# A sum of squares on VectorE: one reduction over nine places in place of two additions in PSUM

## The chip, the cores and the metric

The kernel runs on one core of a Trainium2 chip. The metric is the device time of one execution in microseconds; it is compared by the median of several runs.

## The reference

One layer of a graph network: 12500 nodes with 96 features, 412500 directed edges sorted by their target, four attributes an edge. `_mlp` is a linear layer, ReLU, and a normalization over all rows, whose mean and variance are those of the whole column.

```python
def _mlp(h, W, b, gamma, beta):
    h = jax.nn.relu(h @ W + b)
    mu = jnp.mean(h, axis=0)
    var = jnp.mean(jnp.square(h - mu), axis=0)
    return gamma * (h - mu) * jax.lax.rsqrt(var + EPS) + beta

node_feat = _mlp(x, W_node, b_node, g_node, beta_node)
edge_feat = _mlp(edge_attr, W_edge, b_edge, g_edge, beta_edge)
row, col = edge_index[0], edge_index[1]
message = jnp.concatenate([x[row], x[col], edge_feat], axis=1)
message = _mlp(message, W_msg, b_msg, g_msg, beta_msg)
agg = jax.ops.segment_sum(message, col, num_segments=node_feat.shape[0])
return agg + node_feat          # then x = layernorm(x + this)
```

For the variance of the messages the kernel needs the sum of the squares of all 412500 messages, for each of the 96 features. That sum is what the change touches.

## The kernel before

Edges are handled in groups of 512 (4 tiles of 128 edges, `GT` = 4), and groups in blocks of four (`BG`). Before the main loop, tables are made (`x` times the source and target parts of `W_msg`, as `p_tab` and `q_tab`), the node part is computed and the edge attributes' statistics are taken. The main loop (in `fast`) takes one group at each step `k`; two steps make a pair. All engines' orders in it are written out by hand (`manual_schedule`), so each engine's queue is the order of the code.

A step, by engine:

- GpSimd (POOL) gathers the rows of `p_tab` for a later group, three or four indirect DMAs of 128 rows (`gather`, L226). It reuses the buffer of a pair of groups, and so waits for the pair's second message.
- TensorE (PE) makes the linear part of group `k + 2` into one of three PSUM banks (`linear`, L602, L606), and sums the messages of group `k - 2` by target (`sums`, L666). `edges` (L588) prepares the edge attributes of the next block.
- VectorE (DVE) adds the gathered rows to the linear part and applies the ReLU (`message`, L615, L618, L621). The result `h` lies in SBUF.
- In odd steps ScalarE (ACT) squares the two groups' messages into `sq`, 768 elements a partition (`squared`, L634); `sq` has two buffers, taken in turn. In the same step VectorE adds the squares of the pair *before* (`waiting`) to a running sum of 384 elements a partition in the PSUM bank `mixed` (`moments`, L640), one addition for each of the pair's groups.
- For some groups one of the four tiles is not gathered by GpSimd. Its columns are copied, each by an instruction of its own with an address from a register, out of `x`, which lies in SBUF (`copy_columns`, L745 on VectorE, L747 on ScalarE), into `xc`, and TensorE multiplies them. The addresses are brought into registers by `load_numbers` (L733), one TENSOR_LOAD for up to 20. A pair has three such lots on each of the two engines. VectorE's third lot is loaded between the two additions and copied behind them.
- For some others a tile's rows come by single DMAs from SyncE (SP) (`rows_of`, L433); SyncE also loads the edge attributes and the windows of `q_tab`.

VectorE's queue in an odd step is thus: message, load and copy of the second lot, first addition, load of the third lot, second addition, copy of the third lot. `places_of` (L628) then builds a comparison once a block from `rel` and `nodes_of`, which lies in the same PSUM bank as the running sum, and `add` (L685, L686) takes a finished block's sums over.

The instruction's names: `h` are messages, `z` the linear part, `pa` the sums by target, `pr` and `left` the edge part.

Once, after the loop's last pair, the running sum is reduced over its four tiles to `squares`, 96 elements a partition (L644), and `collect` (L651 to L656) adds what is left on GpSimd, halving the number of places by additions until one is left. A product with ones sums `squares` over the partitions (L839).

Of the kernel before, what the change touches and what calls it, by code (L numbers as in the profile page):

```python
# [12 lines left out]
F32 = mybir.dt.float32  # L13
# [101 lines left out]
def gnn(ctx, tc, t):  # L115
# [147 lines left out]
            for i in range(2):  # L263
                next(store)

    zero = const.tile([64, C], F32, name="zero")
    nc.vector.memset(zero, 0.0)
    nc.sync.dma_start(vec, t["vecs"])
    nc.sync.dma_start(w_node, t["L0_gnn_W_node"])
    nc.sync.dma_start(b_msg, t["L0_gnn_b_msg"])  # L270
# [187 lines left out]
    def fast(ring):  # L458
# [6 lines left out]
                return gather(g, pair[0][:, g % 2, :, :], int(g in by_row or g in by_column))  # L465

        with tc.manual_schedule(engines={ET.SP, ET.Pool}):
            nc.sync.dma_start(q_tab[:WM, :], zero[:WM])
            for r in range(WM + NN, WT, 64):
                n = min(64, WT - r)  # L470
                nc.sync.dma_start(q_tab[r:r + n, :], zero[:n])
            for i in range(2):
                next(store)
            places()
            for i in range(3):
                next(store)
# [12 lines left out]
            for _ in extra:  # L489
                pass  # L490
            got = {g: ahead_of(g) for g in range(SPILL, SPILL + RING)}
        with tc.tile_pool(name="fix", bufs=1) as fix, tc.tile_pool(name="msg", bufs=2) as work, \
                tc.tile_pool(name="msg_ps", bufs=2, space=PSUM) as ps:
            squares = fix.tile([P, C], F32, name="squares")
            mixed = ps.tile([P, GE], F32, name="mixed", bufs=1)
            wide_sq = mixed[:, :GT * C].rearrange("p (t c) -> p t c", c=C)
            nc.vector.memset(wide_sq, 0.0)
            nodes_of = mixed[:, GT * C:GT * C + BG * WN].rearrange("p (k w) -> p k w", w=WN)
            nc.vector.tensor_copy(nodes_of, iota)
            by_place = [ps.tile([P, GE], F32, name=f"pa{i}", bufs=1) for i in range(2)]  # L500
            total = fix.tile([C + 1, 1], F32, name="total")
# [65 lines left out]
            def convert(s):  # L567

                b = order[s]
                px = ps.tile([P, 2, GE], F32, name="pr", bufs=1)  # L570
                for i in range(BG):
                    for k in range(GT):
                        nc.tensor.transpose(px[:C, 0, k * P:(k + 1) * P], got[b * BG + i][:, k, :], ident)
                    xt = work.tile([P, 2, GT, C], F32, name="sq")[:C].rearrange("p g t c -> p (g t c)")[:, :GE]
                    nc.scalar.activation(xt, px[:C, 0, :], AF.Copy)
                    for k in range(GT):
                        nc.tensor.matmul(px[:, 1, k * C:(k + 1) * C], xt[:, k * P:(k + 1) * P], w_msg[:, 0, :],
                                         start=True, stop=True)
                    nc.vector.tensor_copy(got[b * BG + i], px[:, 1, :GT * C].rearrange("p (k c) -> p k c", c=C))
# [50 lines left out]
                    nodes_of[:, :m].unsqueeze(2).to_broadcast([P, m, GT, WN]), op=OP.is_equal)  # L630

            def squared(k, m=2, n=GT):
                sq = work.tile([P, 2, GT, C], F32, name="sq")
                nc.scalar.activation(sq[:, :m, :n, :], hb[k // 2 % HP][:, k % 2:k % 2 + m, :n, :C], AF.Square)  # L634
                return sq

            def moments(sq, at_last, between):

                for i in range(2):
                    nc.vector.tensor_tensor(wide_sq, wide_sq, sq[:, i, :, :], op=OP.add)  # L640
                    if i == 0:
                        between()
                if at_last:
                    nc.vector.tensor_reduce(squares, wide_sq.rearrange("p t c -> p c t"), axis=AX.X, op=OP.add)  # L644

            def collect(x, n, r=P):

                plus = nc.gpsimd.tensor_add
                whole = n if r == P else n - 1
                if r < P:  # L650
                    plus(squares[:r], x[:r, whole * C:n * C], squares[:r])  # L651
                while whole > 1:
                    half = whole // 2
                    plus(x[:, :half * C], x[:, :half * C], x[:, (whole - half) * C:whole * C])
                    whole -= half
                plus(squares, x[:, :C], squares)  # L656
# [69 lines left out]
            def load_numbers(k, part, engine):  # L726

                g, lo, hi = share(engine, k // 2 * XS + part)
                if g is not None:
                    assert engine not in held and hi - lo <= LOADED  # L730
                    if g not in apart:
                        apart[g] = work.tile([C, P], F32, name="xc", bufs=4)
                    _, held[engine] = nc.values_load_multi_w_load_instructions(  # L733
                        numbers[g][:, lo:hi], engines=[engine], min_val=FIRST, max_val=FIRST + 4 * (N - 1),
                        skip_runtime_bounds_check_because="they are nodes' numbers times four bytes, and FIRST")
# [16 lines left out]
            with tc.manual_schedule(engines={ET.SP, ET.Pool, ET.PE, ET.DVE, ET.Activation}):  # L752
# [13 lines left out]
                for k in range(last):  # L766
                    s, g = steps[k]
                    if g % BG == 0:
                        if s + 2 < len(order):
                            load(s + 2)  # L770
                            fetch(s + 2)
                    if k % 2 == 0 and k and pieces:
                        piece(pieces.pop(0))
                    apart_numbers(k)
                    if k % 2 == 0:
                        load_numbers(k, 0, ET.DVE)
                    message(k)
                    load_numbers(k, 1, ET.DVE) if k % 2 else copy_columns(k, 0, ET.DVE)
                    j = k - LATER - BG - 1
                    if k % 2:  # L780
                        load_numbers(k, 1, ET.Activation)
                        copy_columns(k, 1, ET.Activation)
                        now = squared(k - 1)
                        load_numbers(k, 2, ET.Activation)
                        copy_columns(k, 1, ET.DVE)
                        if waiting:
                            moments(waiting, k == last - 1, lambda: load_numbers(k, 2, ET.DVE))
                        waiting = now
                        copy_columns(k, 2, ET.DVE)
                        copy_columns(k, 2, ET.Activation)  # L790
                    if g % BG == 3 and s + 1 < len(order):
                        places_of(s + 1)
                    if j >= 0 and j % BG == 0:
                        add(j // BG, place(j // BG))
                    if k >= LATER:
                        sums(k - LATER)
                    if g % BG != 3 and s + 1 < len(order):
                        if g % 2:
                            edges(s + 1, 1)
                        else:  # L800
                            prepare(s + 1, g % BG // 2)
                    if g % BG == 3:
                        if s + 1 < len(order) and order[s + 1] < RAW:
                            convert(s + 1)
                        if s + 2 < len(order):
                            edges(s + 2, 0)
                    if k + ZB - 1 < n:
                        linear(k + ZB - 1)
                    if k % 2 == 0:
                        load_numbers(k, 0, ET.Activation)  # L810
                        copy_columns(k, 0, ET.Activation)
                    if g >= SPILL:
                        got[ahead] = ahead_of(ahead)
                        ahead += 1
                    apart_rows(k)
                    if k >= (max(column_start) + XN) // XS * 2 + 3 and loads:
                        y0s.append(residual(loads.pop(0)))
# [1 line left out]

                s, g = len(order) - 1, steps[last][1]  # L820
                m, r = NT - (g + 1) * GT, E - (NT - 1) * P
                collect(waiting.rearrange("p g t c -> p (g t c)"), 2 * GT)
                message(last)
                sq = [squared(last, 1, GT)]
                sums(last - 2)
# [1 line left out]
                unread(BUSY - 1)  # L827
                message(n - 1)
                sq.append(squared(n - 1, 1, m))
                collect(sq[0][:, 0, :, :].rearrange("p t c -> p (t c)"), GT)  # L830
                sums(last)
                at_end = place(s - 1), place(s)
                unread(1)
                collect(sq[1][:, 0, :, :].rearrange("p t c -> p (t c)"), m, r)
                add(s - 1, at_end[0])
                sums(n - 1)
                unread(1)
# [242 lines left out]
```

## Time and profile before

| | |
|---|---|
| median of 3 runs | 5507.97 us (5506.36 to 5508.45) |
| the profiled execution | 5517.2 us, its span 5515.5 us |
| mean granted TensorE clock | 0.624 |
| VectorE: busy, instructions | 3251.4 us (59%), 23435 |
| ScalarE: busy, instructions | 2835.6 us (51%), 16834 |
| L640, the additions | 802, 562 ns each |
| L745, VectorE's copies of columns | 20088, 185 ns each, from 1183 to 5363 us |

The profiled execution's time is its span and what lies around it. The page lists busy time, groups of instructions by line, and idle time with what ended it ("releaser"); "issue" is idle time in which an engine waited for nothing that the profile shows. "x20" counts instructions in a row.

### The profile page before, as it was taken

What the parts mean: (1) busy time and instruction counts of PE and PEld (TensorE: products, weight loads), DVE (VectorE), ACT (ScalarE), POOL (GpSimd) and SP (SyncE); (2) the same over time, 40 slices, a digit from 0 to 9 for tenths busy, and PEclk for the clock granted to TensorE, in tenths of its full rate; (3) what the DMA queues carried; (4) which work ended last, traced back from release to release, by engine and by line L of the source; (5) the groups of instructions that cost most, each with busy time, mean ns of one, the idle gap of its engine ahead of it and who ended that gap; (6) DMA issues with size and microseconds to landing.
All of it is one profiled execution on the core that took longest, in us unless ns stands there. A gap on an engine that the chain in (4) does not pass through costs nothing. (4 is left out here: it accounts for less than half of the span.)

```text
span 5515.5 us, 97011 instructions
## 1 busy us (share of the span) xinstructions
PE 3422.6 (62%) x17139; PEld 2745.4 (50%) x17139; DVE 3251.4 (59%) x23435; ACT 2835.6 (51%) x16834; POOL 2773.3 (50%) x2930
## 2 busy tenths in 40 slices
PE   3356674666666665666666666666666666666677
PEld 2133332455555555555555555555555555555556
DVE  1436666135556666666666666666666666666664
ACT  0225553135555565565555555555555655565552
POOL 5644445544445545545545545454555554545454
PEclk6555555565666666666666666666666666666657
DMA  6333332211111111111111111111111111111112
GB/s 165 117 89 70 67 75 64 60 51 29 35 33 40 39 37 42 39 38 39 37 40 32 39 39 40 39 38 39 40 40 40 39 39 38 33 39 39 38 49 83
DMA packets 201728, 274.41 MB, mean 50 GB/s; under 512 B 128941, under 2 KB 132166, under 8 KB 200218
## 3 DMA queue, kind: packets, MB, share of 16 engines
q0 software_dynamic: 92832, 142.78, 10.8%
q1 hardware_dynamic: 95304, 120.39, 7.9%
q10 hardware_dynamic: 12960, 4.93, 0.4%
q14 instruction: 494, 4.05, 0.2%
q8 instruction: 138, 2.26, 0.2%
HBM read 221.63 MB, written 46.23 MB: 49 GB/s over the span
## 5 line engine op out<-in xcount | busy, mean ns | idle before, releaser
L226 POOL DMA_INDIRECT pg<-p_tab,src x2837 | 2690.7, 948 | 2634.1 <-DVE h L621 1230.7
L747 ACT ACTIVATE xc<-big 96x4 uint8 x15624 | 1802.8, 192 | 1357.1 <-issue 1337.3
L745 DVE COPY xc<-big 96x4 uint8 x20088 | 1767.7, 185 | 1076.1 <-issue 1047.4
L602 PE MATMUL z<-rhs,left 128*128 128x96 f32 x6446 | 1449.4, 397 | 1392.9 <-remote 1015.3
L602 PEld LDWEIGHTS z<-rhs,left 128*128 128x128 f32 x6446 | 1318.1, 302 | 1784.5 <-remote 1227.1
L666 PE MATMUL pa<-at,h 128*97 128x80 f32 x6446 | 1005.0, 321 | 42.2 <-issue 42.1
L666 PEld LDWEIGHTS pa<-at,h 128*97 128x97 f32 x6446 | 959.5, 242 | 45.8 <-issue 45.7
L615 DVE CUSTOM_DVE_ANT_0 h<-z,pg 128x384 f32<-128x384 f32 (+1 forms) x690 | 348.2, 505 | 340.0 <-remote 130.1
L588 PE MATMUL pr<-ea,we 7*127 7x512 f32 x1380 | 458.5, 744 | 114.7 <-DMA ea<-rel_d 42.5
L596 ACT ACTIVATE left<-pr 127x1024 f32<-127x1024 f32 x403 | 404.4, 1003 | 236.2 <-remote 130.4
L634 ACT ACTIVATE sq<-h 128x768 f32<-128x768 f32 x404 | 339.7, 841 | 360.7 <-DVE h L621 182.4
L385 PE MATMUL pr<-ea,wide 10*128 10x512 f32 x1212 | 393.3, 1072 | 181.2 <-ACT r L389 80.3
L389 ACT ACTIVATE r<-pr 128x1024 f32<-128x1024 f32 x303 | 291.8, 1025 | 405.4 <-remote 185.9
L640 DVE TENSOR_TENSOR mixed<-mixed,sq 128x384 f32<-128x384 f32 x802 | 451.1, 562 | 82.2 <-DVE mixed L640 64.8
L391 DVE BATCH_NORM_STATS2 estats<-r 128x6 f32<-128x512 f32 x606 | 364.5, 678 | 217.1 <-ACT r L389 112.9
L385 PEld LDWEIGHTS pr<-ea,wide 10*128 10x128 f32 x1212 | 196.3, 322 | 376.8 <-issue 209.4
L588 PEld LDWEIGHTS pr<-ea,we 7*127 7x127 f32 x1380 | 118.1, 208 | 156.3 <-issue 71.8
L628 DVE TENSOR_TENSOR at<-rel,mixed 128x496 f32<-128x496 bf16 x202 | 133.9, 663 | 51.7 <-issue 47.8
L606 PE MATMUL z<-w_msg,xc 96*128 96x96 f32 x558 | 162.1, 390 | 0.0
L606 PEld LDWEIGHTS z<-w_msg,xc 96*128 96x128 f32 x558 | 138.2, 303 | 0.0
L226 POOL DMA_INDIRECT pg<-in_x,src_raw x64 | 60.7, 949 | 62.9 <-DMA spill<-pg 42.7
L357 PE MATMUL py<-center,big 96*128 96x96 f32 x196 | 43.7, 424 | 75.7 <-issue 39.4
(126 smaller groups left out, 868.4 us busy)
## 6 DMA issues: line engine op xcount, KB each, us to landing
rowt<-p_tab SPq DMA_DIRECT2D x5120, 0.4 KB
pg<-p_tab,src POOLq DMA_INDIRECT x2837
pb<-spill SPq DMA_DIRECT2D x29, 768.0 KB
spill<-pg SPq DMA_DIRECT2D x55, 384.0 KB
ea<-in_ea SPq DMA_DIRECT2D x75, 160.0 KB
big<-in_xp SPq DMA_DIRECT2D x28, 336.0 KB
rhs<-q_tab SPq DMA_DIRECT2D x202, 46.5 KB
ea<-in_ea SPq DMA_DIRECT2D x228, 30.0 KB
```

What stands on the lines that cost most here:

```text
L226: made = [nc.gpsimd.indirect_dma_start(out=pg[:, i, :], out_offset=None, in_=tab[:, :], in_offset=bass.IndirectOffsetOnAxis(ap=idx[:, i:i ...
L385: nc.tensor.matmul(pr[:, k % 2, :], wide[Q * i:Q * i + 2 * EK, :], ea[Q * i:Q * i + 2 * EK, b % J, :], start=True, stop=True)
L391: nc.vector.bn_stats(stats[:, (k - o) % NS, (k - o) // NS, :], r[:, 1 - o, :])
L588: nc.tensor.matmul(prs[s, half][:C + WN, i, :], we[o:o + EK + 2, :], block[s][o:o + EK + 2, :], start=True, stop=True)
L596: nc.scalar.activation(x[:C + WN, 2 * half:2 * half + n, :], pr[:C + WN, :n, :], AF.Relu)
L602: nc.tensor.matmul(zb[k % ZB][:, i * C:(i + 1) * C], left[s % 2][:KR, g % BG, i * P:(i + 1) * P], rhs[:KR, s % RB, g % BG, :], start=True, ...
L615: nc.vector._custom_dve(TENSOR_ADD_SAT, out=h[:, :m, :], in0=z[:, :m, :], in1=got.pop(g)[:, :m, :], s0=MOST, s1=0.0)
L634: nc.scalar.activation(sq[:, :m, :n, :], hb[k // 2 % HP][:, k % 2:k % 2 + m, :n, :C], AF.Square)
L640: nc.vector.tensor_tensor(wide_sq, wide_sq, sq[:, i, :, :], op=OP.add)
L666: nc.tensor.matmul(by_place[s % 2][:C + 1, :NW], hb[k // 2 % HP][:r, k % 2, t, :], at[s % AB][:r, i, o + NW * t:o + NW * (t + 1)], start=i ...
L745: nc.vector.tensor_copy(to, x)
L747: nc.scalar.activation(to, x, AF.Copy)
```

## The change

`sq` gets a ninth place of 96 elements behind its eight (two groups of four tiles). `moments` becomes one TENSOR_REDUCE: it reads the nine places of the pair before (eight with squares, the ninth with the sum of all pairs ahead of it), adds them up feature by feature, and writes the 96 sums to the ninth place of the present pair's buffer. For the first pair that place is set to zero. The register load of the third lot, which stood between the two additions, now stands behind the reduction.

With it: the running sum in PSUM is gone, and `nodes_of` moves to the start of its bank; `squares` starts at zero, and the reduction at the loop's end is gone; `collect` takes nine places of the last pair; the tile `zero` is gone, and the rows of `q_tab` that must be zero are written from `shift`, which is zero until the end.

```diff
@@ gnn @@
-    zero = const.tile([64, C], F32, name="zero")
-    nc.vector.memset(zero, 0.0)
@@ fast @@
-            nc.sync.dma_start(q_tab[:WM, :], zero[:WM])
+            nc.sync.dma_start(q_tab[:WM, :], shift[:WM, :C])
...
-                nc.sync.dma_start(q_tab[r:r + n, :], zero[:n])
+                nc.sync.dma_start(q_tab[r:r + n, :], shift[:n, :C])
...
             squares = fix.tile([P, C], F32, name="squares")
+            nc.vector.memset(squares, 0.0)
             mixed = ps.tile([P, GE], F32, name="mixed", bufs=1)
-            wide_sq = mixed[:, :GT * C].rearrange("p (t c) -> p t c", c=C)
-            nc.vector.memset(wide_sq, 0.0)
-            nodes_of = mixed[:, GT * C:GT * C + BG * WN].rearrange("p (k w) -> p k w", w=WN)
+            nodes_of = mixed[:, :BG * WN].rearrange("p (k w) -> p k w", w=WN)
...
             def squared(k, m=2, n=GT):
-                sq = work.tile([P, 2, GT, C], F32, name="sq")
-                nc.scalar.activation(sq[:, :m, :n, :], hb[k // 2 % HP][:, k % 2:k % 2 + m, :n, :C], AF.Square)
+                sq = work.tile([P, 2 * GT + 1, C], F32, name="sq")
+                nc.scalar.activation(sq[:, :m * GT, :].rearrange("p (g t) c -> p g t c", g=m)[:, :, :n, :],
+                                     hb[k // 2 % HP][:, k % 2:k % 2 + m, :n, :C], AF.Square)
                 return sq
 
-            def moments(sq, at_last, between):
-
-                for i in range(2):
-                    nc.vector.tensor_tensor(wide_sq, wide_sq, sq[:, i, :, :], op=OP.add)
-                    if i == 0:
-                        between()
-                if at_last:
-                    nc.vector.tensor_reduce(squares, wide_sq.rearrange("p t c -> p c t"), axis=AX.X, op=OP.add)
+            def moments(sq, to):
+
+                nc.vector.tensor_reduce(to[:, 2 * GT, :], sq.rearrange("p t c -> p c t"), axis=AX.X, op=OP.add)
...
                         if waiting:
-                            moments(waiting, k == last - 1, lambda: load_numbers(k, 2, ET.DVE))
+                            moments(waiting, now)
+                        else:
+                            nc.vector.memset(now[:, 2 * GT, :], 0.0)
                         waiting = now
+                        load_numbers(k, 2, ET.DVE)
                         copy_columns(k, 2, ET.DVE)
...
-                collect(waiting.rearrange("p g t c -> p (g t c)"), 2 * GT)
+                collect(waiting.rearrange("p t c -> p (t c)"), 2 * GT + 1)
```

More of the change, by code (lines that the diff above doesn't have):

```diff
@@ L573, in convert @@
                         nc.tensor.transpose(px[:C, 0, k * P:(k + 1) * P], got[b * BG + i][:, k, :], ident)
-                    xt = work.tile([P, 2, GT, C], F32, name="sq")[:C].rearrange("p g t c -> p (g t c)")[:, :GE]
+                    xt = work.tile([P, 2 * GT + 1, C], F32, name="sq")[:C].rearrange("p t c -> p (t c)")[:, :GE]
                     nc.scalar.activation(xt, px[:C, 0, :], AF.Copy)
@@ L829, in fast @@
                 sq.append(squared(n - 1, 1, m))
-                collect(sq[0][:, 0, :, :].rearrange("p t c -> p (t c)"), GT)
+                collect(sq[0].rearrange("p t c -> p (t c)"), GT)
                 sums(last)
@@ L833, in fast @@
                 unread(1)
-                collect(sq[1][:, 0, :, :].rearrange("p t c -> p (t c)"), m, r)
+                collect(sq[1].rearrange("p t c -> p (t c)"), m, r)
                 add(s - 1, at_end[0])
```

## The prediction

> **What bounds the kernel now.** I read the page first for the span and the engines, then the busy time by stretches to separate the long middle from the ends, then the waits of each engine inside that middle, and last the instructions in order of time.
>
> ```profile
> span 5515.5 us, 97011 instructions
> PE 3422.6 (62%) x17139; PEld 2745.4 (50%) x17139; DVE 3251.4 (59%) x23435; ACT 2835.6 (51%) x16834; POOL 2773.3 (50%) x2930
> ```
> ```profile
> 0.00:1200.00 1200.00, 661.29 (x2399) 404.51 (x2399) 527.01 (x901) 381.83 (x463) 611.48 (x646) 0.55 0.34 85
> 1200.00:5350.00 4150.00, 2642.31 (x14011) 2241.27 (x14012) 2654.91 (x22330) 2409.08 (x16276) 2076.13 (x2196) 0.64 0.15 38
> ```
>
> By busy time nothing is the bound: five engines stand between 50% and 62%. The second fence (columns: PE, PEld, DVE, ACT, POOL) shows where the time is: 4150 us of the 5515 lie in the stretch in which DVE and ACT copy columns of `xc` one by one (L745, L747). There DVE is busy for 2655 us, 64%. What the other 36% wait for decides:
>
> ```profile
> DVE xc L745 <- issue: 1041.9, 1789, 1.5
> DVE h L615 <- issue: 119.0, 205, 1.3
> DVE mixed L640 <- DVE mixed L640: 64.1, 197, 0.7
> DVE pb L579 <- PE pr L577: 45.0, 9, 8.3
> DVE mixed L640 <- issue: 7.3, 15, 1.8
> DVE h L615 <- remote: 9.5, 15, 1.2
> ACT sq L634 <- DVE h L621: 181.9, 235, 3.3
> ACT sq L634 <- DVE h L615: 135.9, 124, 3.9
> POOL pg L226 <- DVE h L621: 1228.2, 239, 36.6
> SPq L716 <- DVEq L733: 187.0, 50, 13.6
> ```
> ```profile
> by line: DVE xc L745 36.2%; issue 31.2%; DVE mixed L640 8.0%; DVE h L615 6.5%; PE z L602 3.9%; PE pr L588 3.9%; PE pa L666 2.5%; DVE at L628 2.2%; DVEq L733 2.1%; DVE h L621 1.3%; SPq L538 1.1%; DVE agg L686 0.6%; DVE h L618 0.5%; DVEq L618
> ```
>
> DVE hardly waits for another engine in this stretch (45.0 us for PE in the `convert` pieces, 9.5 for something unnamed are the largest). It waits for its own issue, 1041.9 us before copies and 119.0 before messages. The others wait for DVE: ACT 181.9 + 135.9 us ahead of its squares, in 359 of some 370 pairs, POOL 1228.2 us before its gathers, SP 187.0 us. The row by itself is the chain of waits for 5248 to 5300 us, the last piece of the stretch that the chain reaches: DVE lines and issue carry most of it, L640 alone 8.0%. So a microsecond that leaves DVE's own queue should leave the time, nearly whole.
>
> The order within two pairs shows how:
>
> ```profile
> 3005.07 0.84 ACT L634 ACTIVATE sq<-h 128x768 f32<-128x768 f32 x1
> 3005.08 0.95 POOL L226 DMA_INDIRECT pg<-p_tab,src  x1 [2.71 <-DVE h L621]
> 3006.87 1.15 DVE L640 TENSOR_TENSOR mixed<-mixed,sq 128x384 f32<-128x384 f32 x2
> 3008.02 11.00 SPq L433 DMA_DIRECT2D rowt<-p_tab  x16
> 3009.43 0.34 DVE L745 COPY xc<-big 96x4 uint8 x1 [0.57 <-issue]
> 3010.84 0.18 DVE L745 COPY xc<-big 96x4 uint8 x1 [0.55 <-issue]
> 3011.55 0.17 DVE L745 COPY xc<-big 96x4 uint8 x1 [0.52 <-issue]
> 3016.47 1.37 DVE L745 COPY xc<-big 96x4 uint8 x18 [0.53 <-issue]
> 3018.45 0.84 ACT L634 ACTIVATE sq<-h 128x768 f32<-128x768 f32 x1 [1.31 <-DVE h L621]
> 3018.47 0.94 POOL L226 DMA_INDIRECT pg<-p_tab,src  x1 [3.68 <-DVE h L621]
> 3019.57 0.55 DVE L640 TENSOR_TENSOR mixed<-mixed,sq 128x384 f32<-128x384 f32 x1
> 3020.39 0.57 DVE L640 TENSOR_TENSOR mixed<-mixed,sq 128x384 f32<-128x384 f32 x1 [0.27 <-DVE mixed L640]
> ```
>
> Each pair has a quick part (18 copies in 1.37 us) and a slow one, in which a copy comes only every 0.71 us (3010.84, 3011.55). The slow part begins some 4 us after POOL starts the burst of gathers that the pair's second message released (3005.08, 3009.43), and ends shortly after that burst (3014.79, which is 3018.47 less 3.68, and 3016.47). The additions lie in the quick part, 1 to 2 us after the message. POOL's burst sets the length of the slow part and idles 3.68 us before the next, so time saved in the quick part shortens the pair one for one: the copies that move forward past the slow part's start had their turn behind its end, where 18 were left.
>
> **The change, part by part.** The main edit is L640. Before, a pair costs DVE two additions of 384 elements and the waits ahead of them:
>
> ```profile
> L640 DVE TENSOR_TENSOR mixed<-mixed,sq 128x384 f32<-128x384 f32 x740 | 416.3, 563 | 80.5 <-DVE mixed L640 64.1 <-issue 7.3
> ```
> ```profile
> L733 DVEq TENSOR_LOAD <-clin x1116: 1094/1234/1368, 1181.3 to 5360.3; - x186
> ```
>
> 740 additions are 370 pairs in the stretch: 416.3 us busy, 64.1 us in which the second addition waits for the first, and 7.3 us of issue, 487.7 us or 1.318 us a pair. The 64.1 us are the register load (L733, median 1234 ns) that stands between the two: begun early in DVE's queue, it ends after the first addition in about half of the pairs (0.27 us late at 3020.39).
>
> After, one TENSOR_REDUCE reads 9 x 96 = 864 elements of `sq` and writes 96. The trace has three such rows near it:
>
> ```profile
> L1030 DVE TENSOR_REDUCE sd<-sq 128x8 f32<-128x768 f32 x12 | 11.2, 939 | 1.5 <-ACT sq L1029 0.9
> L301 DVE TENSOR_REDUCE worst<-rel 128x1 f32<-128x808 bf16 x2 | 2.0, 976 | 0.0
> L644 DVE TENSOR_REDUCE squares<-mixed 128x96 f32<-128x384 f32 x1 | 0.6, 558 | 0.0
> ```
>
> L1030 reads 768 neighbouring f32 elements of SBUF in 939 ns. L644 is the very pattern of the new instruction (96 results, inner step of 96 elements, 384 bytes), but short and out of PSUM: 558 ns for 384. Their difference is 381 ns for 384 elements, 0.99 ns each, so neither the step nor the 96 short sums cost anything there. For 864: at least 939 + 96 x 0.99 = 1034 ns, at most 939 x 864/768 = 1056 ns if all of it grew with the size. I take 1.04 us. This assumes that the step is as free in SBUF as L644 shows it for PSUM, which no row shows; the other end of the bound, one element every second step, is the first rival below.
>
> 370 x 1.04 = 385 us against 487.7: 103 us less. The register load now stands behind the reduction. In the pair shown it held the second addition until 0.82 us after the first had begun (3019.57 to 3020.39); under 1.04 us of reduction it is hidden, so I let the 64.1 us go whole. The 7.3 us of issue lie ahead of whatever comes first and stay: 95 us. From this I take a tenth off, an estimate: SP, which is at its issues for 11.00 us of the pair shown (3008.02), and PE in the `convert` pieces end last now and then. That leaves 86 us.
>
> [...]
>
> Waits: the reduction needs the squares of the pair before, as the first addition does, and its own result of the pair before, long done. Behind it in DVE's queue stand the register load and the third lot of copies, as now. ACT's square of the next pair overwrites the buffer that this reduction reads, and finds it free sooner. The place written lies in the buffer into which ACT writes this pair's squares, but beside them; should it still be made to wait for them, ACT's square ends at 3005.91 and 3019.29, ahead of DVE's 3006.87 and 3019.57. The edges are 0.96 and 0.28 us, so DVE itself would not stand; only the register load could start later.
>
> Outside the stretch lie 34 + 28 additions, 31 pairs. Ahead of it DVE is busy for 527 us of 1200, and behind it the last copies are done; I count nothing for them.
>
> ```profile
> 0.00:1200.00 1200.00, 19.07 (x34) 0.55 0.34 85
> 5350.00:5515.00 165.00, 15.71 (x28) 0.70 0.29 83
> ```
>
>  The memsets, the source of the zeros for `q_tab` (the same DMAs, from a tile zeroed earlier) and the move of `nodes_of` in its bank happen once: nothing. At the end POOL collects nine places in place of eight, and DVE drops L644:
>
> ```profile
> 5467.36 1.16 DVE L640 TENSOR_TENSOR mixed<-mixed,sq 128x384 f32<-128x384 f32 x2
> 5468.47 2.14 POOL L654 TENSOR_TENSOR sq<-sq 128x384 f32<-128x384 f32 x3 [18.31 <-ACT sq L634]
> 5472.98 0.39 POOL L654 TENSOR_TENSOR sq<-sq 128x96 f32<-128x96 f32 x1
> 5473.44 0.39 POOL L656 TENSOR_TENSOR squares<-sq,squares 128x96 f32<-128x96 f32 x1
> 5474.87 0.25 PE L839 MATMUL pa<-ones,squares 128*96 128x1 f32 x2
> ```
>
> One more addition of 0.39 us, and the first now needs the last reduction, which, put where the additions begin (5467.36), ends at 5468.40, no later than POOL starts today. POOL ends at 5473.83 and PE takes the sums up at 5474.87, so 1.0 us of PE's own work covers 0.4. Without that cover it costs 0.4 us. I count nothing.
>
> The sum: 5517.2 us of the profiled execution (span 5515.5) less 86 is 5431; the runs' median is 5508.0, 9 us lower, so the forecast for it is **5422 us**.
>
> **The rivals.** *The step costs in SBUF.* The reduction reads one f32 every 384 bytes, and every row above that reads SBUF takes neighbours, in L301 in runs of four. If each element then takes two steps, the instruction grows by 864 x 0.99 = 0.86 us to 1.90. 370 x 1.90 = 703 us, with the 7.3 us of issue 710: 222 us more than 487.7, all on DVE's queue, since DVE is the bound: 5730. At half that penalty it is 1.47 us and 5508 + 370 x 1.47 + 7.3 - 487.7 = 5572. The change gains below (487.7 - 7.3)/370 = 1.30 us an instruction and loses above. For it: no row of this kernel reads SBUF so. Against it: L644 does in PSUM, at full rate. [...]
>
> *The load stays in sight.* If the register load comes out behind the reduction as it came out between the additions, the 64.1 us stay and 31 remain: 5477. For it: its longest, 1368 ns, exceeds 1040. Against it: it starts ahead of the addition it stands behind.
>
> *The change buys nothing.* The reduction is tied to this pair's squares after all, and the load starts so late that up to 0.25 us a pair come out again, 92 us: about 5508. The order of the rows above (0.28 us to spare) speaks against it.
>
> **How the numbers follow.** The forecast has a chance of 0.50, with its own range of 5400 (the whole 103 us, and some more of issue with it) to 5463 (half passed on). The load in sight has 0.06, nothing gained 0.05, the step in SBUF 0.37, and 0.02 is for something slower that I don't see. A measurement of this kernel tells about 0.2% from no change, 11 us: faster 0.56, same 0.05, slower 0.39. To hold the time 8 times in 10 the range must take in the step's price too, up to two steps an element: 5398 to 5735. I hold the forecast likelier because the one row with the same pattern shows no penalty.
>
> **What would show it.** Right: the new reduction at 1.03 to 1.06 us, 370 of them in the stretch, no wait of DVE behind it, ACT's waits for the messages shorter by about as much as DVE's time, the stretch shorter by some 86 us. Wrong: a reduction of 1.3 us or more, whatever else holds; or one of 1.04 us with DVE's copies behind it waiting for issue, or with SP or PE taking DVE's place in the waits.

## The result, and the profile after

| | before | after |
|---|---|---|
| median of 14 runs each | 5509.3 us (5499.6 to 5546.4) | 5514.6 us (5501.4 to 5535.2) |
| ratio | | 0.9997, interval 0.9983 to 1.0011 |
| profiled execution, span | 5517.2, 5515.5 us | 5513.9, 5512.1 us |

No change that can be measured, where 86 us less had been forecast. (The ratio is formed from all runs; the two medians alone differ by 5 us the other way, which is within it.) The page of the changed kernel (span, busy time by engine):

```profile
span 5512.1 us, 96619 instructions
PE 3460.7 (63%) x17139; PEld 2771.8 (50%) x17139; DVE 3446.4 (63%) x23033; ACT 2836.6 (51%) x16834; POOL 2766.1 (50%) x2931
```

VectorE executes 402 instructions fewer and is busy for 195 us *more*. The groups of instructions (busy us, mean ns of one, idle us ahead of them) say why:

```profile
L637 DVE TENSOR_REDUCE sq<-sq 128x96 f32<-128x864 f32 x401 | 652.3, 1627 | 0.0
L738 DVE COPY xc<-big 96x4 uint8 x20088 | 1764.3, 181 | 1002.3 <-issue 972.4
```

The reduction takes 1627 ns, not 1040. The page lists no wait ahead of it (idle 0.0): the 64.1 us that stood between the two additions are gone. Busy time in the long stretch (PE, PEld, DVE, ACT, POOL):

```profile
1200.00:5350.00 4150.00, 2672.16 (x14026) 2260.99 (x14026) 2838.14 (x21983) 2412.64 (x16289) 2075.74 (x2201) 0.64 0.15 38
```

DVE has 2838.14 us here against 2654.91, and yet POOL issues as many gathers (2201 against 2196), so the stretch moved on as fast. The waits in the same stretch (total us, times, longest):

```profile
DVE xc L738 <- issue: 969.1, 1668, 1.4
DVE h L612 <- issue: 132.1, 217, 1.5
DVE pb L576 <- PE pr L574: 43.5, 9, 7.3
DVE agg L679 <- issue: 42.6, 69, 1.3
POOL pg L226 <- DVE h L618: 1219.0, 239, 36.1
POOL pg L226 <- DVE h L612: 254.0, 72, 4.5
ACT sq L631 <- DVE h L618: 172.2, 237, 2.9
ACT sq L631 <- DVE h L612: 137.6, 124, 3.5
```

DVE works 183 us more in this stretch. Of these, 72.8 us came out of its waits for issue ahead of copies (1041.9 to 969.1), 64.1 us are the wait between the additions, and the rest came out of smaller waits. POOL's waits for the second message are as they were, 239 of them, 5.1 us each. In order of time, one pair:

```profile
3012.62 0.24 DVE L618 TENSOR_SCALAR h<-z 128x96 f32<-128x96 f32 x1
3012.94 1.29 DVE L738 COPY xc<-big 96x4 uint8 x16
3012.97 0.94 POOL L226 DMA_INDIRECT pg<-p_tab,src  x1 [3.18 <-DVE h L618]
3014.14 1.62 DVE L637 TENSOR_REDUCE sq<-sq 128x96 f32<-128x864 f32 x1
3015.68 1.57 DVE L738 COPY xc<-big 96x4 uint8 x20
3019.20 0.94 POOL L226 DMA_INDIRECT pg<-p_tab,src  x1 [0.30 <-issue]
3019.42 0.17 DVE L738 COPY xc<-big 96x4 uint8 x1 [0.50 <-issue]
3020.12 0.17 DVE L738 COPY xc<-big 96x4 uint8 x1 [0.53 <-issue]
3020.84 0.17 DVE L738 COPY xc<-big 96x4 uint8 x1 [0.55 <-issue]
3021.54 0.88 DVE L738 COPY xc<-big 96x4 uint8 x11 [0.53 <-issue]
3023.04 0.94 POOL L226 DMA_INDIRECT pg<-p_tab,src  x1 [2.90 <-DVE h L618]
```

The pair lasts 10.07 us from its first gather to the next pair's (3012.97 to 3023.04). A pair of before that also has six gathers lasted 10.38 us, from 3018.47 to this row:

```profile
3028.85 0.95 POOL L226 DMA_INDIRECT pg<-p_tab,src  x1 [3.19 <-DVE h L621]
```

That is one pair each; the counts of gathers above compare the whole stretch. The slow part (a copy every 0.7 us) is there as before. So two questions: why is the reduction so dear, and why does neither its price nor the saving show in the time?

### The profile page after: what moved, and what is told of

It reads as the page before. It is cut to its first block, busy times and chain, and to the rows that moved or that the text cites. A ratio compares the mean times of both kernels' runs of the same rounds, so it can differ in the third digit from the quotient of the medians.

```text
span 5512.1 us, 96619 instructions
## 1 busy us (share of the span) xinstructions
PE 3460.7 (63%) x17139; PEld 2771.8 (50%) x17139; DVE 3446.4 (63%) x23033; ACT 2836.6 (51%) x16834; POOL 2766.1 (50%) x2931
## 5 line engine op out<-in xcount | busy, mean ns | idle before, releaser
L599 PE MATMUL z<-rhs,left 128*128 128x96 f32 x6446 | 1463.3, 400 | 1367.8 <-remote 1080.5
L599 PEld LDWEIGHTS z<-rhs,left 128*128 128x128 f32 x6446 | 1330.7, 304 | 1768.5 <-remote 1314.7
L637 DVE TENSOR_REDUCE sq<-sq 128x96 f32<-128x864 f32 x401 | 652.3, 1627 | 0.0
L226 POOL DMA_INDIRECT pg<-in_x,src_raw x64 | 60.6, 947 | 64.1 <-DMA spill<-pg 43.9
```

The source lines that it names most:

```text
L226: made = [nc.gpsimd.indirect_dma_start(out=pg[:, i, :], out_offset=None, in_=tab[:, :], in_offset=bass.IndirectOffsetOnAxis(ap=idx[:, i:i ...
L599: nc.tensor.matmul(zb[k % ZB][:, i * C:(i + 1) * C], left[s % 2][:KR, g % BG, i * P:(i + 1) * P], rhs[:KR, s % RB, g % BG, :], start=True, ...
L637: nc.vector.tensor_reduce(to[:, 2 * GT, :], sq.rearrange("p t c -> p c t"), axis=AX.X, op=OP.add)
```

## The experiments

Theories, by the letters of the expectations. **A**: DVE's own time is the bound, as predicted; the dear reduction has eaten the saving. **B**: something else sets the pace, and DVE's work fills its idle time (B1: the register loads). **C**: place decides; work between the end of POOL's burst and the message that releases the next burst counts whole, work in the slow part or near it is hidden. **D**: some 15% of DVE's work counts, wherever it stands. C and D were set up for the last four experiments, after the others had run. Ratios are to the kernel before on the same chip.

### How long the reduction is, and what its length costs

The first set keeps everything but the length. `e1_near` lets the reduction read neighbours, `e2_near2` and `e3_near4` read every element twice and four times, `e0_none` has no reductions.

```diff
# e1_near
-                nc.vector.tensor_reduce(to[:, 2 * GT, :], sq.rearrange("p t c -> p c t"), axis=AX.X, op=OP.add)
+                near = sq.rearrange("p t c -> p (t c)").rearrange("p (c t) -> p c t", t=2 * GT + 1)
+                nc.vector.tensor_reduce(to[:, 2 * GT, :], near, axis=AX.X, op=OP.add)
# e2_near2, e3_near4 (with 4 for 2): as e1_near, but
+                near = near.unsqueeze(2).to_broadcast([P, C, 2, 2 * GT + 1])
+                nc.vector.tensor_reduce(to[:, 2 * GT, :], near, axis=AX.XY, op=OP.max)
# e0_none
-                        if waiting:
-                            moments(waiting, now)
-                        else:
+                        if k == last - 1:
```

> The changed kernel, whose reduction reads nine neighbouring elements for each result instead of nine 384 bytes apart (so it adds up the wrong nine; same count, same waits, same instructions). Both theories: the reduction falls from 1.63 us to 1.03-1.06, if the step is what made it long. Theory A (VectorE's own time is the bound, as predicted): 370 x 0.58 us less than the changed kernel, about 5300 us. Theory B (the time is set by how fast instructions come to VectorE, its register loads above all, and the reduction's length is hidden in idle time): within 25 us of the changed kernel, 5490 to 5535.

> As the first, but every element is read twice, by a step of zero (1728 elements a reduction, the maximum in place of the sum): 1.9-2.0 us each. Theory A: 370 x 0.9 us above the first kernel of this set, +330 us. Theory B: within 40 us of it.

> As before, every element read four times (3456 elements, maximum): 3.7-3.8 us each. Theory A: 370 x 2.7 = +1000 us above the first. Theory B: VectorE has some 3.5 us of idle time a pair in the changed kernel, not all of it where it is needed: +100 to +400 us.

> The changed kernel without the reductions (only the last pairs' squares are summed; all else stays). Theory A: 370 x 1.55 us less than the changed kernel, about 4940 us. Theory B: one instruction a pair less to bring, 0 to 60 us less.

The reductions' rows of `e1_near`, `e2_near2` and `e3_near4`:

```profile
L638 DVE TENSOR_REDUCE sq<-sq 128x96 f32<-128x864 f32 x401 | 416.5, 1039 | 0.0
```
```profile
L639 DVE TENSOR_REDUCE sq<-sq 128x96 f32<-128x1728 f32 x401 | 777.5, 1939 | 0.0
```
```profile
L639 DVE TENSOR_REDUCE sq<-sq 128x96 f32<-128x3456 f32 x401 | 1499.2, 3739 | 0.0
```

Neighbours take 1039 ns: the predicted 1.04 us was right for them, and the step of 384 bytes is the whole difference to 1627 ns. For the time:

| kernel | one reduction | DVE busy in the stretch | DVE's waits for issue before copies | time, ratio (before: 5585.4 us on this chip) |
|---|---|---|---|---|
| `e0_none` | none | 2338 us | 1431.1 us | 5528.3, 0.9897 [0.9859, 0.9935] |
| `e1_near` | 1.04 us | 2619 us | 1135.3 us | 5550.6, 0.9930 [0.9904, 0.9957] |
| `e2_near2` | 1.94 us | 2876 us | 886.5 us | 5591.4, 1.0011 [0.9988, 1.0034] |
| `e3_near4` | 3.74 us | 3371 us | 507.1 us | 5716.1, 1.0245 [1.0206, 1.0284] |

From `e1_near` to `e2_near2` 370 pairs get 0.90 us longer on DVE, 333 us; the time grows by 45 (8.1 thousandths of before's 5585). From there to `e3_near4` 666 us are added, and 131 come out. Only 13% and 20% pass through; from no reduction to 1.04 us it is 18 of 385 us, which is within the noise. Theory A falls. B holds in the main: `e1_near` is 32 to 37 us below the changed kernel, by the ratios, where B allowed 25. Even without any reduction the time is only 1.0% less, some 57 us of 5508, and 78 us at the far end of the interval: with the rest of the kernel as it is, no cheaper way to add the squares would have brought the forecast 86 us. The waits in the stretch show where the rest goes, in `e0_none`:

```profile
DVE xc L738 <- issue: 1431.1, 2319, 3.4
```

and in `e3_near4`:

```profile
DVE xc L740 <- issue: 507.1, 972, 1.3
```

924 us of idle time ahead of copies turn into work. In order of time, `e3_near4`:

```profile
3006.05 0.95 POOL L226 DMA_INDIRECT pg<-p_tab,src  x1 [3.27 <-DVE h L618]
3007.71 3.73 DVE L639 TENSOR_REDUCE sq<-sq 128x96 f32<-128x3456 f32 x1
3011.06 0.95 POOL L226 DMA_INDIRECT pg<-p_tab,src  x1 [0.30 <-issue]
3011.37 1.28 DVE L740 COPY xc<-big 96x4 uint8 x16
3015.38 0.17 DVE L740 COPY xc<-big 96x4 uint8 x1 [0.56 <-issue]
3017.77 0.95 POOL L226 DMA_INDIRECT pg<-p_tab,src  x1 [3.26 <-DVE h L618]
```

The long reduction reaches into the part in which copies came one at a time in the other kernels (from some 4 us after the burst's start), and the 16 copies behind it then run back to back, under POOL's gathers. So the gathers by themselves do not hold a copy up. It looks as if what copies wait for had arrived during the reduction, but no run isolates that. POOL's idle time ahead of its burst is 3.26 us, as in the changed kernel (3.18, 2.90). By the prediction, copies pushed past the slow part's start would get their turn only behind its end; here they catch up within it.

### What a step costs

`e6_steps` is the kernel before with instructions measured ahead of its loop, each four times: reductions of 864 f32 elements of SBUF in nines at steps of 4, 8, 12, 16, 32 and 48 bytes and at 384 as in the change (L499 to L511), of 384 elements of PSUM as neighbours and at 384 bytes (L513, L515), and ACT squares of 768 elements: neighbours, writing at 32 bytes, reading at 48 (L517 to L521). Only these rows are used, not its time.

```diff
+            for i in range(4):
+                nc.vector.tensor_reduce(squares[:C + 1], agg[:, :864 * 4].rearrange("p (c t s) -> p c t s", t=9, s=4)[:, :, :, 0], axis=AX.X, op=OP.add)
...
```

> The kernel before, with reductions of 864 elements ahead of its main loop, read from SBUF in steps of 4, 8, 12, 16, 32, 48 and 384 bytes, four of each, reductions of 384 elements from PSUM in steps of 4 and 384 bytes, and ScalarE's squares of 768 elements written in steps of 4 and 32 bytes and read in steps of 48. If a step costs as soon as two elements don't share 16 bytes: about 1.04 us up to 8 bytes and 1.63 us from 16 (12 between), in SBUF alone; PSUM 0.55 us for both. If it is something else about the changed reduction (its own result as an input, ScalarE writing the other buffer at the time), all of them take 1.04 us.

The groups, by cost:

```profile
L507 DVE TENSOR_REDUCE squares<-agg 97x96 f32<-97x864 f32 x4 | 6.9, 1718 | 0.1
L509 DVE TENSOR_REDUCE squares<-agg 97x96 f32<-97x864 f32 x4 | 6.6, 1650 | 0.1
L505 DVE TENSOR_REDUCE squares<-agg 97x96 f32<-97x864 f32 x4 | 6.5, 1619 | 0.0
L511 DVE TENSOR_REDUCE squares<-agg 97x96 f32<-97x864 f32 x4 | 6.4, 1602 | 0.1
L521 ACT ACTIVATE sq<-agg 96x768 f32<-96x768 f32 x4 | 5.8, 1520 | 0.0
L519 ACT ACTIVATE sq<-agg 96x768 f32<-96x768 f32 x4 | 5.8, 1595 | 0.0
L503 DVE TENSOR_REDUCE squares<-agg 97x96 f32<-97x864 f32 x4 | 5.1, 1278 | 0.0
L501 DVE TENSOR_REDUCE squares<-agg 97x96 f32<-97x864 f32 x4 | 4.2, 1041 | 0.0
L499 DVE TENSOR_REDUCE squares<-agg 97x96 f32<-97x864 f32 x4 | 4.1, 1035 | 0.0
L517 ACT ACTIVATE sq<-agg 96x768 f32<-96x768 f32 x4 | 3.0, 831 | 4.4 <-DVE norm_edge L193 4.4
L513 DVE TENSOR_REDUCE squares<-mixed 128x96 f32<-128x384 f32 x4 | 2.2, 557 | 0.1
L515 DVE TENSOR_REDUCE squares<-mixed 128x96 f32<-128x384 f32 x4 | 2.2, 557 | 0.1
```

In SBUF a step of 8 bytes is free (1041 ns against 1035), 12 bytes cost 0.24 us, and at the four larger steps, 16, 32, 48 and 384 bytes, the reduction takes 1.60 to 1.72 us, 1.55 to 1.66 times as long as with neighbours. In PSUM the step of 384 bytes costs nothing (557 ns both ways), so the row L644, on which the prediction rested, was right and did not bear on SBUF. ACT pays too, in writing at 32 bytes (831 to 1595 ns) and in reading at 48 (1520 ns).

### The register loads

Theory B1: the slow part is set by the loads of copy addresses. The third lot of DVE's copies takes the second lot's addresses, and 372 of the 1116 loads are left out; `e5_act_loads` does so on ACT.

```diff
+                    if engine == ET.DVE and part == 2 and had:
+                        held[engine] = (had * 2)[:hi - lo]
+                        had.clear()
+                        return
...
+                    if engine == ET.DVE and part == 1:
+                        had[:] = val
```

> The changed kernel, whose third lot of copies on VectorE takes the addresses of the second lot and loads none of its own (wrong columns, as many copies; 372 of VectorE's 1116 register loads left out). Theory B1 (VectorE's instructions come too slowly because each register load holds its sequencer for 1.23 us): up to 372 x 1.23 = 458 us less, at least 150, since ScalarE waits for VectorE by only some 310 us in all and becomes the bound after that. Theory A (VectorE's own time): 0 to 20 us less, since its busy time stays.

> The same on ScalarE: its third lot takes the addresses of its second (372 of its 1116 register loads of 0.90 us left out). If VectorE's sequencer alone is the bound: within 30 us of the changed kernel. If the two share the bound (a pair ends when the later of the two is through): 30 to 200 us less.

The chip of this set ran the kernel before in 3736.0 us, not 5508. The ratios are 1.0172 [1.0142, 1.0203] and 1.0169 [1.0138, 1.0200], but the unmodified change was not run there, so what the loads do can't be read from them. The rows of `e6_steps` above come from this chip too. The reduction's own duration doesn't differ: it takes 1627 ns in `e4_dve_loads`, as in the changed kernel elsewhere. In the loop of this chip the slow part is missing; three rows of `e6_steps` in order of time:

```profile
2500.95 0.94 POOL L226 DMA_INDIRECT pg<-p_tab,src  x1 [0.30 <-issue]
2502.19 0.94 POOL L226 DMA_INDIRECT pg<-p_tab,src  x1 [0.30 <-issue]
2502.30 1.56 DVE L769 COPY xc<-big 96x4 uint8 x20 [0.28 <-issue]
```

POOL gathers every 1.25 us almost without a gap, and 20 copies run back to back under its gathers. DVE's idle time ahead of all its copies is 87.5 us here, against 1076.1. The granted clock differs too (0.71 against 0.62), but by far less than the time. `e4b_dve_loads` repeats the kernel on a chip where before takes 5507.9 us, with the changed kernel (`x1_after`) beside it.

> The changed kernel with a third of VectorE's register loads left out (372 of 1116, 1.23 us each; the third lot of copies takes the second's addresses). With the 0.70 us stepping: theory B1 (the loads hold VectorE's sequencer, and that is what bounds) 150 to 450 us below the changed kernel of this set; if the bursts' stepping alone sets the pace, less than 60 us below. Without the stepping: within 1% of the changed kernel.

> The changed kernel once more, beside the three others of this set. Where copies come every 0.70 us during POOL's bursts (the kernel before at some 5500 us): 0.998 to 1.002 of before, as measured. Where that stepping is absent (the kernel before at some 3740 us, as in the previous set), VectorE's time should count for more: theory A's 370 x (1.63 - 1.30) = +120 us there, 1.02 to 1.035.

`x1_after`: 5505.6 us, 0.9988 [0.9974, 1.0002]. `e4b_dve_loads`: 5495.0, 0.9971 [0.9955, 0.9987]. A third of DVE's loads is worth 0.17%, and 0.47% or 26 us with both intervals at their ends, where B1 asked for at least 150 us and the other branch for less than 60. DVE's waits for issue ahead of copies in the stretch stay, too (965.3 us). B1 falls for DVE's loads; leaving out ACT's was not repeated on such a chip.

### POOL's burst

One more gather of 128 rows in each odd group, into a tile of its own, 338 in all, in the kernel before:

```diff
+        if g >= SPILL + RING and g % 2:
+            nc.gpsimd.indirect_dma_start(
+                out=extra_rows, out_offset=None, in_=tab[:, :],
+                in_offset=bass.IndirectOffsetOnAxis(ap=idx[:, 0:1], axis=0))
```

> The kernel before with one more gather of 128 rows in every second group of the main loop (338 more, each 1.25 us of POOL, into a place that nobody reads). If the stepping that goes with POOL's bursts sets the pace of a pair: each burst and its slow part last 1.25 us longer, +200 to +420 us. If not, POOL's idle 3.7 us a pair hide it: 0 to +50 us. Without stepping POOL has hardly any idle time: +300 to +420 us.

5938.8 us, 1.0780 [1.0758, 1.0802]: 431 us, or 1.27 us for each gather. That is the whole of the 1.25 us by which gathers follow each other, although POOL idles some 3 us a pair. POOL's mean wait for a message in the stretch stays: 4.79 us (1114.9 + 240.5 us, 283 times), before 4.78 (1228.2 + 262.6 us, 312 times). So a pair is as long as POOL's burst and the gap behind it, and the gap doesn't give way.

### Where the work stands

`e10_ahead`, the kernel before with both additions ahead of the odd message (the third load goes behind the second lot):

```diff
+                    if k % 2 and waiting:
+                        moments(waiting, k == last - 1, lambda: None)
...
-                        if waiting:
-                            moments(waiting, k == last - 1, lambda: load_numbers(k, 2, ET.DVE))
+                        load_numbers(k, 2, ET.DVE)
```

> The kernel before with its two additions moved ahead of the pair's second message (1.15 us that stand between the end of POOL's burst and the message that releases the next one; the third register load stays behind the second lot). All results as in the reference. Theory C (place decides): 370 x 0.9 to 1.15 us, +330 to +430 us, 1.06 to 1.08 of before. Theory D (15% wherever it stands): 0.995 to 1.01.

5831.9 us, 1.0588 [1.0560, 1.0616]: 324 us more for the same two additions, 0.87 us a pair. In order of time:

```profile
3012.04 1.16 DVE L640 TENSOR_TENSOR mixed<-mixed,sq 128x384 f32<-128x384 f32 x2
3013.10 0.55 DVE L615 CUSTOM_DVE_ANT_0 h<-z,pg 128x384 f32<-128x384 f32 x1
3013.92 0.95 POOL L226 DMA_INDIRECT pg<-p_tab,src  x1 [4.58 <-DVE h L615]
```

The additions end, the message follows, and POOL starts behind it, after 4.58 us of idling where pairs of before had 2.71, 3.68 and 3.19. The stretch says the same: POOL's mean wait for a message goes from 4.78 us (1228.2 + 262.6 us, 312 times) to 5.74 (1368.9 + 297.1 us, 290 times).

```profile
POOL pg L226 <- DVE h L621: 1368.9, 224, 34.4
POOL pg L226 <- DVE h L615: 297.1, 66, 5.0
```

Theory D is out here. C's mechanism held, with the time just short of its range (324 us where it gave 330 to 430). At 1.15 us a pair the additions are 425 us of DVE's time: the move brings out 76% of them beyond what they cost in the old place.

`e11_behind` puts the changed kernel's reduction behind the third lot of copies. `e12_even` takes `e0_none` and puts a reduction of 1.95 us (of `rel`, its result unused) behind the pair's *first* message.

```diff
# e11_behind
+                        load_numbers(k, 2, ET.DVE)
+                        copy_columns(k, 2, ET.DVE)
                         if waiting:
                             moments(waiting, now)
...
-                        load_numbers(k, 2, ET.DVE)
-                        copy_columns(k, 2, ET.DVE)
# e12_even
+                    if k % 2 == 0:
+                        nc.vector.tensor_reduce(squares, rel.rearrange("p g t -> p (g t)")[:, :18 * C].rearrange("p (c t) -> p c t", t=18), axis=AX.X, op=OP.max)
```

> The changed kernel with the reduction (1.63 us, step of 384 bytes) moved behind the third lot of copies, to the end of the odd step, nearer to the slow part. All results as in the reference. Theory C: its length is hidden as good as wholly, 0.988 to 0.995 of before, near to the kernel without reductions (0.990). Theory D: as the changed kernel, 0.998 to 1.002.

> The kernel without reductions of the squares, with a reduction of 1728 two-byte neighbours that nobody uses (1.9 to 2.0 us) behind each pair's first message, in the slow part. Theory C: hidden, 0.988 to 0.996 of before (without any reduction 0.990; the same length in the old place 1.001). If the slow part ends before it and it pushes the copies that are left towards the second message: above 1.01.

`e11_behind`: 5508.3 us, 1.0002 [0.9985, 1.0020], nothing gained. `e12_even`: 5575.2, 1.0121 [1.0094, 1.0148], which is 2.2% or 123 us over `e0_none`. Its row:

```profile
L772 DVE TENSOR_REDUCE squares<-rel 128x96 f32<-128x1728 bf16 x402 | 782.8, 1947 | 50.0 <-issue 41.6
```

1.947 us in 370 pairs are 720 us, of which 17% come out: as much as behind the second message (13 to 20%). C's main branch missed in both, and D held in `e11_behind`. For `e12_even` the expectation had a second branch, above 1.01 if copies are pushed towards the second message, and that is the number that came. POOL's mean wait for the second message is 5.3 us there (1269.1 us, 239 times) where the changed kernel has 5.1, which fits. But PE waited for this reduction, 455.6 us ahead of its products for `z` (L599), and the granted clock was 0.606 against 0.622, so how its price came through is not shown, and `e0_none` ran on another chip.

Each theory thus holds for one half. Ahead of the message that releases POOL, the work counts nearly whole, as C had it; at the places tried behind a message, about a sixth of it does, as D had it.

### A version that beats both

Squares are stored feature by feature, nine places together. The reduction then reads neighbours; ACT writes at a step of 36 bytes, and the last pair is collected by one more reduction in place of POOL's additions.

```diff
-                sq = work.tile([P, 2 * GT + 1, C], F32, name="sq")
-                nc.scalar.activation(sq[:, :m * GT, :].rearrange("p (g t) c -> p g t c", g=m)[:, :, :n, :],
-                                     hb[k // 2 % HP][:, k % 2:k % 2 + m, :n, :C], AF.Square)
+                sq = work.tile([P, C, 2 * GT + 1], F32, name="sq")
+                if m == 2:
+                    to = sq[:, :, :2 * GT].rearrange("p c (g t) -> p g t c", g=2)
...
+                nc.scalar.activation(to, hb[k // 2 % HP][:, k % 2:k % 2 + m, :n, :C], AF.Square)
...
-                nc.vector.tensor_reduce(to[:, 2 * GT, :], sq.rearrange("p t c -> p c t"), axis=AX.X, op=OP.add)
+                nc.vector.tensor_reduce(to[:, :, 2 * GT], sq, axis=AX.X, op=OP.add)
...
-                collect(waiting.rearrange("p t c -> p (t c)"), 2 * GT + 1)
+                nc.vector.tensor_reduce(squares, waiting, axis=AX.X, op=OP.add)
```

> The changed kernel with the squares stored feature by feature: ScalarE writes each square 36 bytes from the one before, VectorE's reduction reads nine neighbours. All results as in the reference. If ScalarE's write costs nothing by its step: reduction 1.03-1.06 us, 0.5 to 0.9% less than before (theory B, from the kernel with neighbours, 0.993), 4% less by theory A. If the step costs ScalarE as much as VectorE (0.84 to 1.4 us), the gain is gone: within 0.3% of before or slower.

> The changed kernel with the squares stored feature by feature, ScalarE writing in steps of 36 bytes, VectorE's reduction reading neighbours. From the steps measured in the previous set: reduction 1.04 us in place of 1.63, ScalarE's square 1.60 in place of 0.84. With the stepping: between the kernel with neighbours alone (0.993 of before) and 1.003. Without it: 0.995 to 0.999, as measured.

> Both at once: squares stored feature by feature (reduction 1.04 us, ScalarE's square 1.58 us) and the reduction behind the third lot of copies. All results as in the reference. Theory C: the reduction's length no longer counts in that place, so within 0.3% of the kernel with the step of 384 bytes in the same place, or up to 0.3% slower by ScalarE's longer square. Theory D: 0.992, as with the old place.

On the chip without a slow part, `e9_ct` has 3723.9 us, 0.9970 [0.9954, 0.9986]. On the others `e9b_ct`, the same kernel, has 5465.5, 0.9919 [0.9905, 0.9933], and `e13_ct_behind` (with its reduction behind the third lot too) 5463.1, 0.9914 [0.9888, 0.9940], as D had it and not C. `e9b_ct` came out slightly below its range of 0.993 to 1.003. The groups of `e9b_ct`:

```profile
L635 ACT ACTIVATE sq<-h 128x768 f32<-128x768 f32 x404 | 637.0, 1577 | 221.4 <-DVE h L611 99.9
L640 DVE TENSOR_REDUCE sq<-sq 128x96 f32<-128x864 f32 x401 | 417.3, 1041 | 0.0
```

ACT's square takes 1577 ns, 736 ns more than the 841 of the changed kernel, and the time is still 0.7% less than `x1_after`. At the place where ACT squares, it used to wait for messages, 309.8 us in the rows above and 175.3 here. So about half of the 272 us that the longer squares take in 370 pairs comes out of these waits, and 74.9 us more out of ACT's waits for issue ahead of its copies (1335.2 to 1260.3).

## Why the prediction was wrong

**The bound.** "A microsecond that leaves DVE's own queue should leave the time, nearly whole": this step failed first. It took the others' waits for DVE as proof that all of DVE's time is on the path. Those waits are for *messages*. `e10_ahead` shows that time ahead of the message counts (the additions cost 324 us more there), `e2_near2`, `e3_near4` and `e12_even` that elsewhere 13 to 20% count, where nine tenths were taken. The sentence further down, that the copies that move forward past the slow part's start "had their turn behind its end", is where it went astray: the rows of `e3_near4` show the 16 copies behind 3.73 us of reduction catching up back to back. The prediction itself read DVE's 1041.9 us of waits for issue; it did not ask whether new work could fill them.

**The size of the reduction.** 1.04 us was taken, 1627 ns measured. The row L644 lay in PSUM, where the step of 384 bytes costs nothing (557 ns both ways); out of SBUF the reduction took 1.6 times as long with it (1627 against 1039 ns). This term of the sum was mis-sized: 370 x 1.04 = 385 us came out as 602. The prediction named this gap and chose the nearer row by pattern, not by memory. The first rival, the step in SBUF, was right that the step costs there, at two thirds of its size (0.59 us of the 0.86 that it added). Its two steps an element were the author's estimate: no run shows them; the steps from 16 bytes on cost 1.55 to 1.66 times as much as neighbours (`e6_steps`). Its time was wrong: by its formula 1.627 us give 5508 + 370 x 1.627 + 7.3 - 487.7 = 5630 us, for it shared the failed bound. The rival "The change buys nothing" had the right time, about 5508, by luck: it rested on a tie to the pair's own squares and on a late register load, and neither is in the trace (idle 0.0 ahead of the reduction, and the copies behind the one at 3014.14 follow without a gap at 3015.68).

**What met.** The second addition's wait is gone, and no wait for the reduction's own buffer came in its place (idle 0.0 ahead of L637). Neighbours reduce in 1039 ns, as worked out.

**The sum as it is.** With the reduction at 1.04 us the change gains 0.70% (`e1_near`), 39 us of 5508. These are 38% of the 103 us that leave DVE's queue by the prediction's sum (23 to 51% by the interval), which is more than a sixth; what the register load's new place adds to it was not measured alone. As written the change gains nothing (0.9988 and 0.9997), and the version with neighbours, in which ACT's squares and the last collection differ too, is 40 us faster than it on the same chip (5465.5 against 5505.6). So the step costs some 40 us, 18% of the 217 us by which DVE's reductions get longer (370 x 0.586), and that is what the change gains otherwise. "No change" is a gain and a loss of the same size. No run shows a reason why they should be so nearly equal; it is taken for chance.

**What stays open.** Why a copy comes only every 0.7 us in the slow part, and why one chip (3736 us) doesn't have it; taking away a third of DVE's loads didn't change it. Whether instructions reach DVE late was not tested. Why a sixth of DVE's time elsewhere passes through. And what the change itself does on that chip. There DVE is busy for 82% of the span (`e6_steps`), but POOL's gathers, one every 1.25 us, alone fill 2837 x 1.25 = 3546 of its 3758 us. The two ratios of 1.017 there are of kernels with fewer loads, so the change as written may be slower there; it wasn't run.

## What to carry to other kernels

"Others wait for engine X" points first at those instructions of X that release them; here only work ahead of them carried the time nearly whole (324 of the additions' 425 us in `e10_ahead`). So put a suspected cost ahead of the release, or double it behind, before pricing the whole engine's time. Where an engine waits for issue between its own instructions, as DVE did here for 1041.9 us ahead of copies, new work can be partly free (here 13 to 20% of what was added behind the message reached the time), and so a saving there partly worthless. And before an access with a large step goes into an inner loop, take its price from the memory that it reads: here a VectorE reduction of f32 elements of SBUF 16 to 384 bytes apart took 1.55 to 1.66 times as long as one of neighbours (1602 to 1718 ns against 1035), and a ScalarE square written at 32 bytes or read at 48 took 1.9 and 1.8 times (1595 and 1520 ns against 831). Lay the data so that the engine with time to spare pays.

## What the runs showed of the hardware

- The kernel before took some 5508 us in three sets of runs, 5585 us in one and 3736 us in one, on different chips. Three instructions last as long at 5508 as at 3736 (a square of ACT 841 ns on both, a gather 948 and 945 ns, the changed reduction 1627 ns on both); what differs in the order of time is whether copies run back to back under POOL's gathers (DVE idles 1076.1 us ahead of its copies at 5508, 87.5 at 3736).
- PSUM read by VectorE at a step of 384 bytes: a reduction of 384 f32 elements takes 557 ns, as with neighbours.
- In SBUF a reduction's price by its step (864 f32 elements) rises between 8 and 16 bytes: 1035 ns for neighbours, 1041 at 8 bytes, 1278 at 12, 1619 at 16, then 1718, 1650 and 1602 at 32, 48 and 384.
